# A graph layer's row picks by one-hot products: the one-hots as the moving side, the node table as the stationary one

## The chip, the cores and the metric

The kernel runs on one core of a Trainium2 chip. The metric is the device time of one execution in microseconds; three runs of the kernel before took 2540.1, 2541.27 and 2552.49 us, median 2541.27 us. The profile is of one more execution. Its columns name the engines: PE is TensorE's matmul, PEld TensorE's weight load, DVE VectorE, ACT ScalarE, POOL GpSimd, SP SyncE (which here only issues DMAs). A small q behind an engine's name is its queue of instructions, where waits and DMA issues stand.

## The reference

One message-passing layer on a graph with 6250 nodes and 206250 edges, 64 channels in 4 heads of 16, with a residual and a normalisation. The edges come sorted by destination.

```python
def reference(x, src, dst, edge_attr_64, Wq, bq, Wk, bk, We, be, Wv, bv):
    Qh = (x @ Wq.T + bq).reshape(n, H, D)
    Kh = (x @ Wk.T + bk).reshape(n, H, D)
    Vh = (x @ Wv.T + bv).reshape(n, H, D)
    Ee = (edge_attr_64 @ We.T + be).reshape(-1, H, D)
    score = (Kh[src] * Qh[dst] * (1.0 / np.sqrt(D)) * Ee).sum(-1)
    score = jnp.exp(jnp.clip(score, -5.0, 5.0))
    msg = Vh[src] * score[..., None]
    wV = jax.ops.segment_sum(msg, dst, num_segments=n).reshape(n, H * D)
    return _layernorm(x + wV, axis=-1)
```

## The kernel before

**Tiling.** An edge tile is 128 edges, one to a partition; 8 tiles are a group, 2 groups (16 tiles) a step. There are 105 steps: 97 of two groups and 8 of one group at the end. A step needs, for each edge, the key and value of its source node (128 numbers), the query of its destination node (64 numbers) and its edge term.

**Set-up.** Keys, values and queries of all nodes are computed once. Keys and values go to a table in DRAM (`kv_tab`), the queries, each split into three bf16 parts whose sum is the float32 value, to another (`q3_tab`). The node features themselves stay in SBUF as `parts`, also in three bf16 parts (call them high, middle and low), as 50 blocks of 128 nodes.

**Keys and values of an edge** come in two ways. Most tiles are gathered: GpSimd issues an indirect DMA per tile that fetches 128 rows of `kv_tab` (`gather_kv`, L443), four steps ahead of use into a ring of five steps' buffers. `gather` (L573) releases a step's gathers in six portions: a small copy of the source indices (`due_i`, L584 on VectorE or L586 on ScalarE) stands at a chosen place in that engine's order, and the gathers wait for it. Two tiles of each step, and three of every fifth (`THIRD`), 213 in all, are *picked* instead: their node features are taken out of `parts` by matmuls with one-hots, and then multiplied with the key and value weights. Picking a tile two steps ahead takes, in the names of the code:

- `sources` (L500, ScalarE): source index minus 50 times the column number, so that the number of the block appears in the column that belongs to the node's partition; `sources_turned` (L506, TensorE) transposes it into a PSUM bank, the tile `small`.
- `hots` (L516, VectorE): compares it with 25 block numbers at a time and writes one-hots, 25 blocks x 128 edges, two instructions per tile.
- `picks` (L530, TensorE): for each of the 50 blocks, a weight load of the one-hot (128 x 128) and a matmul that moves the 192 columns of the block's three parts past it; the 50 add up in PSUM (`rows3`, in the bank `pick`).
- `picked` (L544, VectorE) adds the three parts and copies out; `picked_turned` (L551, TensorE; L554, ScalarE) transposes; `picked_kv` (L564 to L571) multiplies with the weights, adds the bias by a matmul, and ScalarE copies the result into the ring.

**Queries of an edge** are spread by one-hots as well. Since edges are sorted by destination, the destinations of a group lie in a window of 42 nodes; `fetch_queries` (L187) loads that window's rows (42 nodes x 3 parts = 126 rows), `spread` (L594, TensorE) repeats the group's row of destination keys over the partitions into PSUM by two matmuls of 512 columns, `onehot_rows` (L616) and `onehot_rows_rest` (L621) make one-hots of it on ScalarE, and `queries` (L639) multiplies. Destination one-hots of the other kind (`onehot_edges`, L629) serve to add up the messages.

**One step** then runs: products (L646, L647) of keys, queries and edge terms on VectorE; scores (L653, L655, L656); messages (L663); a split of the messages into three bf16 parts, ScalarE copying a part (L666, L676) and TensorE subtracting it (`minus`, L674), twice; in the next step sixteen matmuls add the messages up by destination (`sums`, L682), and VectorE adds the result into a ring of accumulators (L696). Edge terms are eight float32 matmuls per step (`edge_values`, L432) onto a bias that ScalarE writes (L608).

**What sets the order.** Nothing is moved by a scheduler: every engine works off its instructions in the order in which the body of the loop over steps (L759 to L825) calls the functions above, and waits by semaphores where a tile is not ready or not free. The picks' work of a step is strewn over that body, so that TensorE has something between the links of the chain products, scores, messages, subtractions. PSUM's eight banks are all given out: `small`, `pick`, two each for `pe`, `pq` and `pb` (the spread keys, or a place for picked rows). Buffers for one-hots of picks: five.

## Time and profile before

| | us |
|---|---|
| median of three runs | 2541.27 |
| the profiled execution | 2551.2 |
| its span, first to last instruction | 2549.4 |
| set-up, to the first products | 134.2 |
| 97 steps of two groups begin between | 134.2 and 2443.9 |

The page gives busy times of each engine over the span; "by line" groups give the summed busy time, the mean of one instruction in ns and, behind the second bar, the engine's idle time just ahead of the group's instructions with what ended it. "Issue" there means that nothing the profile shows ended it, "remote" that a semaphore did whose setter could not be told. Rows of the windows' view read: stretch in us, its length, then busy us and number of instructions of PE, PEld, DVE, ACT and POOL, the granted share of TensorE's clock, the mean busy share of the DMA engines, and GB/s. Rows of the timeline read: start and duration in us, engine, line, operation, what is written and read, shape, number of instructions merged, and the idle time before it. Rows of the waits' view read: total us, times, longest.

### The profile page before, as it was taken

The numbers are of one execution on the slowest core, as the hardware profiler recorded it, in microseconds if no ns is written. First come the engines' busy times: TensorE is split into PE (matmuls) and PEld (weight loads), VectorE is DVE, ScalarE is ACT, GpSimd is POOL, SyncE is SP. The second block draws the span as 40 slices with busy tenths as digits, with TensorE's granted clock in tenths as the row PEclk, the third lists the DMA queues.
The fourth block names the chain that finished last, engine by engine and source line by source line (L and its number), as shares of the span: only waits on it lengthen the run. The fifth ranks groups of instructions, "written<-read, shape, count | busy, mean of one in ns | idle before, by whom it ended". The sixth has DMA issues, their size and how long they took to land.

```text
span 2549.4 us, 42602 instructions
## 1 busy us (share of the span) xinstructions
PE 1964.5 (77%) x17255; PEld 1623.3 (64%) x17255; DVE 1632.6 (64%) x2106; ACT 1029.6 (40%) x1778; POOL 1321.2 (52%) x1411
## 2 busy tenths in 40 slices
PE   4577877778877888777788787778778777777874
PEld 4466766666666666666666666667666666666663
DVE  3466766667666566676666666766767566666764
ACT  1344443434434344344343443444434343343544
POOL 5345555555555555555555555555555555555542
PEclk9988888988989888888888898888888898889985
DMA  4412222222222222222222222222222222222221
GB/s 119 125 41 66 56 67 63 59 65 65 65 57 54 65 65 58 72 65 57 64 66 55 64 58 66 62 60 56 70 69 56 64 68 55 66 62 55 64 57 35
DMA packets 104940, 163.05 MB, mean 64 GB/s; under 512 B 67130, under 2 KB 67454, under 8 KB 104622
## 3 DMA queue, kind: packets, MB, share of 16 engines
q0 software_dynamic: 44768, 90.73, 13.6%
q1 hardware_dynamic: 59582, 68.51, 9.5%
q8 instruction: 137, 2.24, 0.4%
q10 hardware_dynamic: 384, 1.00, 0.2%
q14 instruction: 69, 0.57, 0.1%
HBM read 152.79 MB, written 7.33 MB: 63 GB/s over the span
## 4 chain that ended last, share of the span: by engine, by line
PE 50%; issue 19%; POOL 10%; another core or an unknown queue 6%; DVE 5%; ACT 5%; DMA 0%; POOLq 0%; DVEq 0%; ACTq 0%
PE pick L530 25%; POOL kv L443 10%; PE pe L432 6%; PE pq L674 4%; PE pb L530 3%; PE small L682 3%; PE pb L594 2%; PE pb L566 2%; PE pq L639 2%; ACT msg L676 2%; DVE prod L646 1%; DVE prod L647 1%; DVE small L653 1%; PE pb L551 1%
## 5 line engine op out<-in xcount | busy, mean ns | idle before, releaser
L443 POOL DMA_INDIRECT kv<-kv_tab,due_i x1340 | 1263.7, 943 | 1149.3 <-DVE due_i L584 423.4
L530 PEld LDWEIGHTS <-hot 128*128 128x128 bf16 x10650 | 1002.3, 107 | 504.4 <-issue 431.7
L530 PE MATMUL pick<-parts,hot 128*128 128x192 bf16 x9700 | 1035.8, 265 | 298.7 <-issue 205.9
L516 DVE TENSOR_TENSOR hot<-small,block 128x3200 bf16<-128x3200 bf16 x426 | 755.5, 1815 | 18.4 <-remote 6.3
L616 ACT ACTIVATE to<-pb,minus_row 126x1024 bf16<-126x1024 f32 x202 | 224.0, 1109 | 842.4 <-PE pb L594 412.9
L646 DVE TENSOR_TENSOR prod<-kv,pq 128x1024 f32<-128x1024 f32 (+2 forms) x105 | 123.7, 1178 | 421.5 <-issue 148.6
L676 ACT ACTIVATE msg<-pq 128x1024 bf16<-128x1024 f32 (+2 forms) x210 | 207.2, 987 | 167.6 <-PE pb L551 81.4
L432 PEld LDWEIGHTS pe<-we_sb,et 128*128 128x128 f32 x1612 | 210.6, 207 | 86.1 <-ACT pe L608 64.2
L432 PE MATMUL pe<-we_sb,et 128*128 128x128 f32 x1612 | 226.2, 295 | 44.0 <-ACT pe L608 33.1
L621 ACT ACTIVATE to<-to,one_p 126x1024 bf16<-126x1024 bf16 x202 | 230.2, 1139 | 0.1
L682 PE MATMUL small<-msg,of 128*128 128x192 bf16 x1612 | 178.0, 262 | 33.2 <-issue 31.9
L544 DVE TENSOR_REDUCE xp<-pick 128x128 f32<-128x384 f32 x97 | 53.7, 554 | 203.7 <-remote 174.4
L674 PE MATMUL pq<-msg,minus_b 128*128 128x512 bf16 x404 | 132.7, 407 | 57.3 <-ACT msg L676 49.4
L682 PEld LDWEIGHTS <-of 128*128 128x128 bf16 x1612 | 146.6, 104 | 47.4 <-issue 45.2
L653 DVE TENSOR_REDUCE small<-prod 128x64 f32<-128x1024 f32 (+2 forms) x105 | 123.9, 1180 | 76.5 <-remote 34.6
L594 PE MATMUL pb<-key_rows,ident_b 112*128 112x512 bf16 x403 | 138.2, 423 | 23.9 <-ACT to L616 12.4
L530 PE MATMUL pb<-parts,hot 128*128 128x192 bf16 x950 | 116.7, 287 | 31.3 <-issue 31.1
L647 DVE TENSOR_TENSOR prod<-prod,pe 128x1024 f32<-128x1024 f32 (+2 forms) x105 | 123.6, 1177 | 4.0
L663 DVE TENSOR_TENSOR pq<-kv,small 128x1024 f32<-128x1024 f32 (+2 forms) x105 | 123.5, 1176 | 0.2 <-ACT small L656 0.2
L629 DVE TENSOR_TENSOR of<-small,key 128x2048 bf16<-128x2048 bf16 (+2 forms) x105 | 123.1, 1172 | 0.3
L571 ACT ACTIVATE kv<-pb 128x256 f32<-128x256 f32 (+1 forms) x97 | 39.2, 404 | 172.6 <-PE pb L566 51.7
L666 ACT ACTIVATE msg<-pq 128x1024 bf16<-128x1024 f32 (+2 forms) x105 | 103.8, 988 | 1.4 <-DVE pq L663 1.4
(140 smaller groups left out, 1321.1 us busy)
## 6 DMA issues: line engine op xcount, KB each, us to landing
et<-in_eT SPq DMA_DIRECT2D x100, 512.0 KB
kv<-kv_tab,due_i POOLq DMA_INDIRECT x1340
qw<-q_tab SPq DMA_DIRECT2D x202, 15.8 KB
kv_tab<-kv_sb SPq DMA_DIRECT2D x5, 640.0 KB
q_tab<-q SPq DMA_DIRECT2D x5, 480.0 KB
acc<-in_x SPq DMA_DIRECT2D x48, 32.0 KB
out<-y SPq DMA_DIRECT2D x48, 32.0 KB
xT_sb<-in_xT ACTq DMA_DIRECT2D x3, 320.0 KB
```

The costliest lines, as they stand in the source:

```text
L432: nc.tensor.matmul(pe[:, 2 * u:2 * u + 2, :], et[:, u, :], we_sb, start=False, stop=u == n // 2 - 1, skip_group_check=True)
L443: nc.gpsimd.indirect_dma_start(out=kv_of(g)[:, j, :], out_offset=None, in_=kv_tab[:, :], in_offset=bass.IndirectOffsetOnAxis(ap=of[:, t:t ...
L516: nc.vector.tensor_tensor(HOT[s, i, h].rearrange("p b (a c) -> p b a c", c=2), pairs(from_b[i])[:, None].to_broadcast(shape), block2[:, bl ...
L530: nc.tensor.matmul(to, hot[:, k, :], parts[:, b], start=b == 0, stop=b == NB - 1)
L594: nc.tensor.matmul(pb[:, b:b + 4, :], ident_b[:NR2, g // 2:g // 2 + 1].to_broadcast([NR2, P]), key_rows[:, g % 2, b * P:(b + 4) * P], star ...
L616: nc.scalar.activation(TO[g][:, :n, :], pb[:3 * W, :n, :], AF.Square, bias=minus_row3[:3 * W])
L621: nc.scalar.activation(TO[g][:, :n, :], TO[g][:, :n, :], AF.Relu, bias=one_p[:3 * W], scale=-1.0)
L646: nc.vector.tensor_mul(prod[:, :n, :], kvs[s % KVB][:, :n, :C], PQ[s][:, :n, :])
L653: nc.vector.tensor_reduce(score, prod[:, :n, :].rearrange("p g (h d) -> p g h d", h=H), axis=AX.X, op=OP.add)
L674: nc.tensor.matmul(msg[:, lo:hi, :], minus_b, M3[s][:, lo:hi, i, :], start=False, stop=True, skip_group_check=True)
L676: nc.scalar.activation(M3[s][:, :n, i + 1, :], msg[:, :n, :], AF.Copy)
L682: nc.tensor.matmul(PA[s], OH[s][:, j, :], M3[s][:, j], start=j == 0, stop=j == n - 1)
```

## The change

Picks are made for four tiles at a time, a batch of two steps' tiles, and the operands of the matmul change places.

- For each of the 50 blocks the stationary side is now a 128-column slice of `parts`, and the moving side the one-hots of all four tiles, 512 columns. Two matmuls per block: one whose slice holds the high and middle parts (into the bank `hi_mid`), one whose slice begins at the low part (into `low`; the upper 64 rows of that result, the next block's high part, are not read). A 51st block of zeros pads the table.
- The result has channels on the partitions and edges along the columns, which is how the next product needs it. So the reduction over the parts (L544) and the transposes (L551) go; ScalarE copies both banks out every second step (`picked`), and `picked_kv` multiplies, tile by tile, by weights stacked twice (`w2`: high and middle are added by the product itself) and by weights with the bias as a 65th row (`wb`). These are float32 matmuls.
- `hots` now writes 5 blocks x 512 edges; ten instructions per batch, five per step. `picks` runs in five portions per step, ten matmuls each.
- Batches run 0 to 46 (steps 0 to 93), three steps ahead: 188 tiles are picked, always the last two of a step; every-fifth-step thirds are gone.
- `spread` goes: the rows of destination keys are written to a DRAM table once (`key_tab`), and `fetch_keys` on SyncE's queue loads each group's row, repeated over 126 partitions, into one of four SBUF buffers two steps ahead. `onehot_rows` reads that.
- The sixth portion of a step's gathers is released by VectorE in place of ScalarE, and later in the body. The bank pair `pb` is given to `room`, where the picked keys and values are made, and `low`.
- In the other branch, which this input does not take, a tile of zeros is smaller.

The diff, without the parts that only rename or only touch set-up of tiles:

```diff
-LAST = NS - 8 - 1
+AHEAD = 3
+BATCH = 4
+LAST = (NS - 8 - AHEAD) // 2
+CUTS = 5
+NC = NB // CUTS // 2
...
+    key_tab = dram.tile([NR2, 2 * G * P], BF16, name="key_tab")
...
+            nc.sync.dma_start(key_tab, key_rows.rearrange("p i e -> p (i e)"))
...
+            def sources(m):
+                if m < LAST:
+                    for i in range(BATCH):
+                        FAR[m, i] = work.tile([P, P], BF16, name="far", bufs=BATCH)
+                        nc.scalar.activation(FAR[m, i], row50, AF.Identity, scale=-1.0,
+                                             bias=src_f[:, 2 * m + i // 2, i % 2:i % 2 + 1])
...
+            def hots(s, c):
+                if picks_in(s):
+                    b0 = (s % 2 * NC + c) * CUTS
+                    HOT[s, c] = work.tile([P, CUTS, BATCH * P], BF16, name="hot", bufs=5)
+                    shape = [P, CUTS, BATCH * P // 2, 2]
                     nc.vector.tensor_tensor(
-                        HOT[s, i, h].rearrange("p b (a c) -> p b a c", c=2),
-                        pairs(from_b[i])[:, None].to_broadcast(shape),
-                        block2[:, blocks(h), None, :].to_broadcast(shape), op=OP.is_equal)
+                        HOT[s, c].rearrange("p b (a c) -> p b a c", c=2),
+                        pairs(from_b)[:, None].to_broadcast(shape),
+                        block2[:, b0:b0 + CUTS, None, :].to_broadcast(shape), op=OP.is_equal)
...
-                    for k in range(NB // 2):
-                        b = h * NB // 2 + k
-                        nc.tensor.matmul(to, hot[:, k, :], parts[:, b], start=b == 0,
-                                         stop=b == NB - 1)
+                    for k in range(CUTS):
+                        b = (s % 2 * NC + c) * CUTS + k
+                        for i, to in ((0, hi_mid), (2, low)):
+                            at = (3 * b + i) * C
+                            nc.tensor.matmul(to, parts_flat[:, at:at + 2 * C], hot[:, k, :],
+                                             start=b == 0, stop=b == NB - 1)
...
             def picked(s):
-                if picks_in(s):
-                    X[s] = work.tile([P, 3, C], F32, name="xp")
-                    nc.vector.tensor_reduce(X[s][:, 1:], rows3.rearrange("p k i c -> p k c i"),
-                                            axis=AX.X, op=OP.add)
+                if s % 2 and picks_in(s):
+                    nc.scalar.activation(x2, hi_mid, AF.Copy)
+                    nc.scalar.activation(x1[:C], low[:C], AF.Copy)
+
+            def picked_kv(s, i):
+                if s % 2 and picks_in(s):
+                    to = s - 1 + AHEAD + i
+                    n = tiles_in(to)
+                    for j in range(2):
+                        es = slice((2 * i + j) * P, (2 * i + j + 1) * P)
+                        nc.tensor.matmul(rooms[:, j], x2[:, es], w2, start=j == 0, stop=False,
                                          skip_group_check=True)
+                        nc.tensor.matmul(rooms[:, j], x1[:, es], wb, start=False, stop=j == 1,
+                                         skip_group_check=True)
+                    nc.scalar.activation(kvs[to % KVB][:, n - 2:n, :], rooms, AF.Copy)
...
-                    if part < 3:
+                    if part not in (3, 4):
                         nc.vector.tensor_copy(due_i[:, due], src_i[:, due])
...
-            def spread(g):
-                pb = psum.tile([P, G, P], F32, name="pb")
-                for b in range(0, tiles_of(g), 4):
-                    nc.tensor.matmul(pb[:, b:b + 4, :],
-                                     ident_b[:NR2, g // 2:g // 2 + 1].to_broadcast([NR2, P]),
-                                     key_rows[:, g % 2, b * P:(b + 4) * P], start=True, stop=True)
-                return pb
+            def fetch_keys(g):
+                n = tiles_of(g) * P
+                KB[g] = work.tile([3 * W, G * P], BF16, name="kb", bufs=4)
+                nc.sync.dma_start(KB[g][:, :n], key_tab[g // 2:g // 2 + 1, g % 2 * G * P:][:, :n]
+                                  .to_broadcast([3 * W, n]))
...
+            def onehot_rows(g):
                 n = tiles_of(g)
                 TO[g] = work.tile([3 * W, G, P], BF16, name="to", bufs=4)
-                nc.scalar.activation(TO[g][:, :n, :], pb[:3 * W, :n, :], AF.Square,
-                                     bias=minus_row3[:3 * W])
+                nc.scalar.activation(TO[g][:, :n, :],
+                                     KB.pop(g)[:, :n * P].rearrange("p (j e) -> p j e", j=n),
+                                     AF.Square, bias=minus_row3[:3 * W])
```

and the body of the loop, with the calls in their new order (unchanged calls that stand between are left in):

```diff
                 if s + 2 < NS:
                     for g in groups_of(s + 2):
                         fetch_queries(g)
+                        fetch_keys(g)
                 if s:
                     sums(s - 1)
-                sources_turned(s, 1)
-                sources_turned(s + 1, 0)
-                sources_turned(s, 2)
+                picked(s - 1)
                 prod = products(s)
                 gather(s + KVB - 1, 0)
-                picked(s - 1)
-                picked_third(s - 1)
                 if more:
-                    onehot_rows(nexts[0], spread(nexts[0]))
-                picks(s, 0, 0)
+                    onehot_rows(nexts[0])
+                picks(s, 0)
                 score = scores(s, prod)
...
-                hots(s, 1, 0)
-                picks(s, 0, 1)
-                picked_turned(s - 1)
+                hots(s, 2)
+                picks(s, 1)
+                picked_kv(s - 1, 0)
                 minus(s, msg, 1)
                 gather(s + KVB - 1, 4)
...
-                hots(s, 1, 1)
-                picks(s, 1, 0)
-                picked_kv(s - 1)
-                gather(s + KVB - 1, 5)
-                sources(s + 1, 1)
-                sources(s + 2, 0)
-                sources(s + 1, 2)
+                hots(s, 3)
+                picks(s, 2)
+                if s % 2 == 0:
+                    sources((s + 2) // 2)
+                picked_kv(s - 1, 1)
+                hots(s, 4)
                 if more:
                     onehot_edges(s + 1)
                     queries(s + 1)
-                picks(s, 1, 1)
-                for h in range(2):
-                    hots(s, 2, h)
-                for h in range(2):
-                    picks(s, 2, h)
-                hots(s + 1, 0, 0)
-                hots(s + 1, 0, 1)
+                if s % 2:
+                    sources_turned((s + 1) // 2)
+                picks(s, 3)
+                hots(s + 1, 0)
+                gather(s + KVB - 1, 5)
+                picks(s, 4)
+                hots(s + 1, 1)
```

More of the change, by code (lines that the diff above doesn't have):

```diff
@@ L459, in tile_gnn @@
                 tc.tile_pool(name="psum", bufs=1, space=bass.MemoryType.PSUM) as psum:
-            TO, OH, PE, PQ, M3, PA = ({} for _ in range(6))
+            TO, OH, PE, PQ, M3, PA, KB = ({} for _ in range(7))
             small = fixed.tile([P, 4 * P], F32, name="small")
-            col, *from_b = (small[:, i * C:(i + 1) * C].bitcast(BF16) for i in range(4))
+            from_b = small[:, :4 * C].bitcast(BF16)
             score_all = small[:, 4 * C:4 * C + 2 * G * H]
             pa = small[:, 5 * C:8 * C].rearrange("p (i c) -> p i c", i=3)
+            room = fixed.tile([P, 4 * P], F32, name="room")
@@ L482, in tile_gnn @@
-            pick = fixed.tile([P, 4 * P], F32, name="pick")
-            rows3 = pick[:, :6 * C].rearrange("p (k i c) -> p k i c", k=2, i=3)
+                nc.vector.tensor_copy(src_f[:, :, i],
+                                      src_i[:, t0 + i:t0 + i + 2 * G * (2 * LAST - 1) + 1:2 * G])
+            hi_mid = fixed.tile([P, 4 * P], F32, name="pick")
+            low = fixed.tile([P, 4 * P], F32, name="low")
+            x2 = accp.tile([P, 4 * P], F32, name="x2")
+            x1 = accp.tile([C + 1, 4 * P], F32, name="x1")
@@ L504, in sources_turned @@
-            def sources_turned(s, i):
-                if wanted(s, i):
-                    nc.tensor.transpose(from_b[i], FAR.pop((s, i)), ident_b)
-            def blocks(h):
-                return slice(h * NB // 2, (h + 1) * NB // 2)
-            def hots(s, i, h):
-                if wanted(s, i):
-                    HOT[s, i, h] = work.tile([P, NB // 2, P], BF16, name="hot", bufs=5)
-                    shape = [P, NB // 2, P // 2, 2]
-                    nc.vector.tensor_tensor(
-                        HOT[s, i, h].rearrange("p b (a c) -> p b a c", c=2),
-                        pairs(from_b[i])[:, None].to_broadcast(shape),
-                        block2[:, blocks(h), None, :].to_broadcast(shape), op=OP.is_equal)
@@ new lines, in sources_turned @@
+            def sources_turned(m):
+                if m < LAST:
+                    for i in range(BATCH):
+                        nc.tensor.transpose(from_b[:, i * P:(i + 1) * P], FAR.pop((m, i)), ident_b)
+            def hots(s, c):
[3 more added lines that the diff above has]
+                    shape = [P, CUTS, BATCH * P // 2, 2]
+                    nc.vector.tensor_tensor(
+                        HOT[s, c].rearrange("p b (a c) -> p b a c", c=2),
+                        pairs(from_b)[:, None].to_broadcast(shape),
+                        block2[:, b0:b0 + CUTS, None, :].to_broadcast(shape), op=OP.is_equal)
@@ L578, in gather @@
                 lo, hi = PARTS[part] * n // 16, PARTS[part + 1] * n // 16
-                todo = [t for t in range(t0 + lo, t0 + hi) if not is_picked(t // G, t % G)
-                       ]
+                todo = [t for t in range(t0 + lo, t0 + hi) if not is_picked(t // G, t % G)]
                 if todo:
                     due = slice(todo[0], todo[-1] + 1)
-                    if part < 3:
+                    if part not in (3, 4):
                         nc.vector.tensor_copy(due_i[:, due], src_i[:, due])
@@ L744, in tile_gnn @@
             closed, scaled, normed = 0, 0, 0
-            sources(0, 0)
-            sources_turned(0, 0)
+            for g in range(4):
+                fetch_keys(g)
+            sources(0)
+            sources_turned(0)
             keys(0)
             for k, g in enumerate(groups_of(0)):
-                onehot_rows(g, spread(g))
+                onehot_rows(g)
                 onehot_rows_rest(g)
@@ L753, in tile_gnn @@
             onehot_edges(0)
-            sources(0, 1)
-            sources(1, 0)
-            sources(0, 2)
-            for h in range(2):
-                hots(0, 0, h)
+            for c in range(2):
+                hots(0, c)
             for s in range(NS):
```

97 lines of the change are left out of this document (24 added, 73 removed).

## The prediction

> **What bounds the kernel now.** I read the page first: busy shares, then the chain that ended last.
>
> ```profile
> span 2549.4 us, 42602 instructions
> PE 1964.5 (77%) x17255; PEld 1623.3 (64%) x17255; DVE 1632.6 (64%) x2106; ACT 1029.6 (40%) x1778; POOL 1321.2 (52%) x1411
> PE 50%; issue 19%; POOL 10%; another core or an unknown queue 6%; DVE 5%; ACT 5%; DMA 0%; POOLq 0%; DVEq 0%; ACTq 0%
> ```
>
> TensorE leads, but a fifth of the chain is "issue": an engine that waits for nothing the profile shows. How long is a step? One line's own view, and the timeline at the 97th step:
>
> ```profile
> L646 DVE TENSOR_TENSOR prod<-kv,pq x105: 421/1221/1223, 134.2 to 2536.2; 128x1024 f32<-128x1024 f32 x97, 128x512 f32<-128x512 f32 x7, 128x256 f32<-128x256 f32 x1
> 2443.87 1.21 DVE L646 TENSOR_TENSOR prod<-kv,pq 128x1024 f32<-128x1024 f32 x1
> ```
>
> 96 steps in 2443.9 - 134.2 = 2309.7 us: 24.06 us each, with 134 us ahead and 105.5 us of tail. Now the busy times by window; the counts behind the first two columns are TensorE's matmuls and weight loads:
>
> ```profile
> 134.20:2443.90 2309.70, 1835.74 (x16540) 1520.76 (x16540) 1525.75 (x1816) 947.22 (x1578) 1227.06 (x1302) 0.88 0.23 62
> 1226.60:1234.60 8.00, 6.94 (x49) 5.72 (x49) 5.35 (x10) 5.10 (x6) 3.53 (x4) 0.81 0.11 33
> 1230.20:1238.20 8.00, 7.07 (x68) 5.88 (x66) 7.76 (x11) 6.26 (x9) 5.67 (x6) 1.00 0.37 107
> 1238.20:1240.90 2.70, 0.82 (x7) 0.31 (x5) 2.66 (x2) 0.00 (x0) 0.94 (x1) 1.00 0.19 49
> 1251.90:1259.90 8.00, 7.27 (x59) 6.72 (x60) 2.57 (x7) 2.03 (x3) 0.63 (x1) 0.68 0.00 1
> 1258.60:1266.60 8.00, 7.93 (x78) 6.74 (x76) 7.76 (x11) 6.59 (x9) 5.65 (x6) 1.00 0.16 43
> 1266.60:1269.00 2.40, 0.79 (x6) 0.28 (x4) 2.40 (x2) 0.00 (x0) 0.94 (x1) 1.00 0.21 55
> ```
>
> 8 us with 134 instructions end in 2.7 us with 12; 8 us with 154 end in 2.4 us with 10; stretches with 98 and 119 run on. Over the loop TensorE takes 33080 / 2309.7 = 14.3 instructions per us, 345 a step. My reading: it can be fed some 14 to 15 per us for long, and what a burst takes above that it pays back in a pause. The pause spreads:
>
> ```profile
> 1219.06 2.23 PE L530 MATMUL pick<-parts,hot 128*128 128x192 bf16 x25
> 1221.13 1.48 PE L682 MATMUL small<-msg,of 128*128 128x192 bf16 x16
> 1226.12 0.56 DVE L544 TENSOR_REDUCE xp<-pick 128x128 f32<-128x384 f32 x1 [3.81 <-remote]
> 1226.73 3.65 PE L530 MATMUL pick<-parts,hot 128*128 128x192 bf16 x25 [2.95 <-issue]
> ```
>
> Picks recorded as done at 1221.3 are told to VectorE at 1226.1 only. Its reduction (L544) starts then, the next picks wait for it, and run at half rate: 3.65 us in place of 2.23, since the granted clock has fallen. The mean clock of 0.88 is a consequence, as is much of what the other engines' rows call "remote": they wait for TensorE's word, not for its work. So a step of 24.06 us is three things on TensorE: its streams of columns, the pauses, and the half clock after them; VectorE (15.9 us busy a step) and GpSimd follow.
>
> **The change, part by part** (per step unless said). Costs by group:
>
> ```profile
> L530 PEld LDWEIGHTS <-hot 128*128 128x128 bf16 x10650 | 1002.3, 107 | 504.4 <-issue 431.7 <-DVE prod L646 0.6
> L530 PE MATMUL pick<-parts,hot 128*128 128x192 bf16 x9700 | 1035.8, 265 | 298.7 <-issue 205.9 <-DVE xp L544 87.6 <-DVE prod L647 2.3
> L516 DVE TENSOR_TENSOR hot<-small,block 128x3200 bf16<-128x3200 bf16 x426 | 755.5, 1815 | 18.4 <-remote 6.3 <-issue 5.2 <-PE pick L530 3.3
> L629 DVE TENSOR_TENSOR of<-small,key 128x2048 bf16<-128x2048 bf16 x97 | 117.9, 1215 | 0.3
> L544 DVE TENSOR_REDUCE xp<-pick 128x128 f32<-128x384 f32 x97 | 53.7, 554 | 203.7 <-remote 174.4 <-PE pb L594 24.1 <-PE pick L530 3.6
> L594 PE MATMUL pb<-key_rows,ident_b 112*128 112x512 bf16 x403 | 138.2, 423 | 23.9 <-ACT to L616 12.4 <-issue 11.3
> L674 PE MATMUL pq<-msg,minus_b 128*128 128x512 bf16 x402 | 131.9, 408 | 54.6 <-ACT msg L676 48.9 <-issue 5.2 <-ACT msg L666 0.6
> L432 PEld LDWEIGHTS pe<-we_sb,et 128*128 128x128 f32 x1612 | 210.6, 207 | 86.1 <-ACT pe L608 64.2 <-issue 17.7 <-ACT to L621 0.3
> L443 POOL DMA_INDIRECT kv<-kv_tab,due_i x1340 | 1263.7, 943 | 1149.3 <-DVE due_i L584 423.4 <-issue 332.2 <-ACT due_i L586 326.3
> 1213.13 0.59 PE L674 MATMUL pq<-msg,minus_b 128*128 128x512 bf16 x2
> 1218.06 0.70 PE L566 MATMUL pb<-wkv,xe 128*128 128x256 f32 x2
> 1218.60 0.63 PE L639 MATMUL pq<-qw,to 126*128 126x64 bf16 x16
> 1222.62 0.94 POOL L443 DMA_INDIRECT kv<-kv_tab,due_i  x1 [0.30 <-issue]
> 1231.81 2.05 PE L432 MATMUL pe<-we_sb,et 128*128 128x128 f32 x16 [0.93 <-ACT pe L608]
> ```
>
> *Instructions of TensorE.* 10650 picks were 97 x 110; 47 batches x 100 are now 50 a step (94 steps). In load-and-multiply pairs: out go 110 picks, 4 spreads, 2 transposes of sources and some 5 of the transpose and key/value work; in come 50, 2, and 8 (four fp32 matmuls, two records each, as L432's 16 for eight show). 345 - 242 + 120 = 223. At 14.3 per us that is 15.6 us: no longer the bound. How fast is the feed without bursts? The trace bounds it only by this mean, which has the pauses in it, and from below by the 119 / 8 = 14.9 of the stretch that ran on. At 12 per us the 223 would still take 18.6, less than the sum below, so the choice within these bounds moves little. A batch's picks, two instructions per 0.22 us, come at 9 per us; bursts are left in sums, queries and edges, 32 instructions each.
>
> *Columns of TensorE.* From 25 and 16 matmuls of 192 columns: (2.23 - 1.48) / 9 = 0.083 us each, so 0.222 for 512 columns; two in 0.59, less one of 0.41, say 0.18. I take 0.222, the longer run. Picks: 50 x 0.222 = 11.1 (9.0 at 0.18) against 110 x 0.083 = 9.1: **dearer by 2.0**. The four spreads go (0.9). Key/value: four fp32 matmuls at 2.05 / 8 = 0.26 make 1.0, about what the bias matmul, L566's pair and the transposes took. Sum: picks 11.1, sums 16 x 0.083 = 1.3, queries 0.6, edges 2.05, minus 1.0, key/value 1.0, transposes 0.1 = 17.2 at full clock; the same for before, 16.1.
>
> The Trainium skill ("TensorE: Matmul & The Clock Gate", Back-to-back issue gap) gives about 216 ns for an isolated 512-column matmul but 131 ns sustained; at 131 the picks would be 6.6. No row here shows under 180, so the trace speaks for its first figure.
>
> The second matmul of each block computes 64 rows that nobody reads (the next block's first part), which is why 4/3 of the columns are paid for; the wider moving side saves weight loads that ran beside the multiplies anyway.
>
> *VectorE.* A one-hot of 2560 elements, between 2048 (1.215) and 3200 (1.815): 1.48; five make 7.4. Out: (755.5 + 53.7) / 97 = 8.3. One copy of indices comes over from ScalarE (0.2). Busy 1525.75 / 96 = 15.9 becomes 15.2. L544 no longer stands between picks and picks. What is late next on this engine is the chain products, scores, ScalarE's exponential, message: in order as before, and scores still wait for the sums, which share a bank with them. The four transposes of a batch's sources stand on TensorE behind the queries and wait for VectorE's fifth one-hot of the odd step; VectorE has then only the edges' one-hots (1.2 us) left before it needs their result, which the transposes, 0.3 us, meet. I take 0, from 0 to that 1.2 every second step.
>
> *GpSimd.* A gather takes 0.94 + 0.30 = 1.25 us. 188 tiles are picked in place of 213, so 14 gathers a step: **17.5 us** (17.3 before, hidden in 24). This becomes the tightest floor. The sixth release of indices moves from ScalarE behind VectorE's one-hots of the next step; behind it stands one more one-hot, and the copy waits for nothing, so its price is the 0.2 above.
>
> *ScalarE and the queues:*
>
> ```profile
> L676 ACT ACTIVATE msg<-pq 128x512 bf16<-128x512 f32 x14 | 8.4, 597 | 12.6 <-PE pq L674 12.6
> L571 ACT ACTIVATE kv<-pb 128x256 f32<-128x256 f32 x78 | 29.9, 383 | 144.1 <-PE pb L566 51.7 <-PE pq L639 42.1 <-PE pick L530 19.1
> L616 ACT ACTIVATE to<-pb,minus_row 126x1024 bf16<-126x1024 f32 x201 | 223.3, 1111 | 840.0 <-PE pb L594 410.6 <-remote 372.2 <-PE pick L530 41.9
> L621 ACT ACTIVATE to<-to,one_p 126x1024 bf16<-126x1024 bf16 x201 | 229.5, 1142 | 0.1
> 1219.12 1.08 SPq L187 DMA_DIRECT2D qw<-q_tab  x2
> DVE prod L646 <- DMA kv<-kv_tab,due_i: 39.7, 12, 6.4
> ```
>
> Every second step two evacuations of 512 columns, 2 x 0.6, of which the reading of hi_mid must be over before the next batch's first pick. Behind them on ScalarE stand the one-hots of the next step. On TensorE the sums (1.3 us) cover them; without that cover they cost 0.6 a step; I take 0.2. The four source rows of a batch now come in one step in place of two in each; ScalarE stays near 947.22 / 96 = 9.9, idle more than half the time, and that hides them. The squares read SBUF and wait for TensorE no more (L616's 410.6): 1.14 for 1.11. The keys' DMAs: two more issues on SyncE, some 1.1 us, two steps ahead, into buffers that ScalarE emptied a step before; behind them stands only the next step's loading. 252 packets of 2 KB, 516 KB a step, are as much again as the edges' loads, on a mean DMA share of 0.23. I take nothing, since waits for a gather's landing come to 39.7 us in the whole run (last row); the upper end is in rival 3. Start: a table written and read back before the first one-hots, +3 us (0 to 10), and three gathers more in a queue that has slack there.
>
> **Sum.** TensorE 17.2. Waits for others that stay: (64.2 + 48.9) / 97 = 1.2; the evacuation 0.2; pauses left over from short bursts (sums and queries together still come at over 14 per us), taken as a tenth of (431.7 + 205.9) / 97 = 6.6, i.e. 0.6. Bounds of the three: 0 to 2.5 for the waits (L544's 87.6 of picks' idle goes, but a like wait could come), 0 to 0.6, and 0 to 6.6; I stay near the low ends, since the counts above leave the bursts short and scattered. **19.2 us a step**, above GpSimd's 17.5. Between the marks of step 0 and step 96 are 94 steps with picks and two without (13 us each, an estimate: eight gathers at 1.25 and the chain of products and messages). In the tail step 96 picks no more, 2.5 us less. Span: 137 + 94 x 19.2 + 26 + 103 = 2071; in general 266 + 94 T. The profiled run is 2551.2, 2 above its span and 10 above the median of 2541.27, so the forecast is **2075**, about 18% off.
>
> **Rivals.**
> 1. *Pauses are not tied to the number of instructions.* For it: the profile names no releaser, and a load of edges or a run of gathers often lies near. Then pauses and cold clock stay and the columns cost: (17.2 - 16.1) / 0.88 = 1.25 more a step, 25.3: 266 + 94 x 25.3 = **2645, slower**. It decides if pauses come in 8-us stretches with fewer than 120 instructions. Against it: the windows above. A rule on its side: the Trainium skill ("Runtime: NRT & Kernel Launch", Instruction fetch mechanics) holds that fetching is hidden by an issue floor of some 20 cycles, so that the count would not matter. Chance 0.09.
> 2. *GpSimd's floor.* The pauses vanish with their waits, T = 17.5 to 18.2: **1911 to 1977**. For it: TensorE's 17.2 lies just below. Against it: gathers are released piecemeal by copies on VectorE and ScalarE (423.4 + 326.3 us of idle). Chance 0.15.
> 3. *Half the pauses stay,* or the keys' DMAs bring a like loss: +3 us, T = 20.3 to 23.3, middle **2315**. Chance 0.19.
> 4. *Nothing comes of it:* a new wait eats the gain, within 0.5% of 2541. Chance 0.03.
>
> **How the numbers follow.** Forecast (T 18.2 to 20.3, 1977 to 2174): 0.54. The range takes in the upper 0.7 of rival 2 (T from 17.7) and the lower 0.8 of rival 3 (T to 22.7): 1930 to 2400, which holds 0.54 + 0.11 + 0.15 = 0.8. Measurements of this kernel tell about 0.5% from no change. Faster: 0.54 + 0.15 + 0.19 = 0.88; same 0.03; slower 0.09.
>
> **What would show it.** Right: L530's idle by "issue" under 100 us; granted clock above 0.95; some 223 TensorE instructions a step; picks 0.22 apart; GpSimd above 60% busy. Wrong: pauses of 0.7 us and more inside the picks' runs; picks cold at 0.43; one-hots waiting for the keys' DMA; key/value products waiting for late gathers.

## The result, and the profile after

The kernel after took 2463.76 us (median of four, 2458.75 to 2469.47) against 2546.88 us before (four, 2540.1 to 2554.36): ratio 0.967, 95% interval 0.963 to 0.972. Faster, as foreseen, but by 3.3% where 18% was foreseen, and above the range. In three later sets of runs, one on another chip and two on a chip that gave the long times in other sets, the kernel before took about 1790 us; the kernel after, run in one of them, took 1988 us, a ratio of 1.112 (1.107 to 1.116): there the change is a loss. One execution of the kernel before in the last of these sets took 2368.39 us, at a granted clock of 0.66 where its other executions have 0.97; it is left out of that set's ratios.

First the page of the kernel after, from the set of the 0.967:

```profile
span 2457.0 us, 30837 instructions
PE 1852.5 (75%) x11184; PEld 1101.6 (45%) x11184; DVE 1504.8 (61%) x2122; ACT 1034.2 (42%) x1627; POOL 1345.5 (55%) x1436
issue 24%; PE 20%; POOL 16%; ACT 15%; another core or an unknown queue 12%; DVE 10%; DMA 2%; DVEq 0%; POOLq 0%; SPq 0%; ACTq 0%
L518 PE MATMUL pick<-hot,parts 128*128 128x512 bf16 x2350 | 937.8, 399 | 3.8 <-issue 3.8
L506 DVE TENSOR_TENSOR hot<-small,block 128x2560 bf16<-128x2560 bf16 x470 | 679.4, 1481 | 337.6 <-PE small L498 250.1
L518 PEld LDWEIGHTS <-parts 128*128 128x128 bf16 x4700 | 473.0, 102 | 581.7 <-issue 120.7
```

TensorE's pauses inside the picks are nearly gone: 3.8 us of idle by issue on the multiplies and 120.7 on the loads, where L530 had 205.9 and 431.7. Yet the chain has more issue than before, and no engine is busy for more than 75%. The windows' row of the 96 steps between the first and the 97th product:

```profile
147.22:2359.41 2212.19, 1730.15 (x10614) 1004.82 (x10613) 1403.25 (x1843) 951.80 (x1435) 1248.19 (x1323) 0.93 0.32 88
```

A step takes 2212.19 / 96 = 23.04 us, for 24.06 before. TensorE is busy for 18.02 of it (19.12 before) and idle for 5.02 (4.94 before). So only the busy part shrank, with the granted clock up from 0.88 to 0.93; the pauses' time came back as waits. Which ones, the waits' view says; five of its rows (total us, times, longest):

```profile
DVE hot L506 <- PE small L498: 250.1, 34, 9.0
ACT x L524 <- PE pick L518: 238.7, 35, 8.3
ACT msg L639 <- remote: 235.9, 57, 6.3
PE pq L637 <- ACT msg L639: 137.8, 44, 4.2
PE pe L431 <- ACT pe L571: 118.6, 45, 10.1
```

Three of the five are ScalarE or VectorE waiting for TensorE. (Of these, the second is no sign of trouble: in run c_after, told below, it is 268.3, while the first is 107.9 there.) The third close up, in the timeline (rows of TensorE, ScalarE and GpSimd):

```profile
1205.85 0.59 PE L637 MATMUL pq<-msg,minus_b 128*128 128x512 bf16 x2
1208.23 0.38 PE L518 MATMUL low<-hot,parts 128*128 128x512 bf16 x1
1209.23 1.02 ACT L639 ACTIVATE msg<-pq 128x1024 bf16<-128x1024 f32 x1 [3.61 <-remote]
1205.92 0.95 POOL L442 DMA_INDIRECT kv<-kv_tab,due_i  x1 [0.30 <-ACT to L584]
1207.17 0.94 POOL L442 DMA_INDIRECT kv<-kv_tab,due_i  x1 [0.30 <-issue]
1210.62 0.94 POOL L442 DMA_INDIRECT kv<-kv_tab,due_i  x1 [2.50 <-ACT due_i L551]
```

The second subtraction ends at 1206.44, and TensorE goes on: the pick at 1208.23 is the tenth that it starts behind it. ScalarE, idle since 1205.6, begins the copy at 1209.23, 2.8 us later. TensorE's word (the update of its semaphore, by which the others learn that a result is there) came late: the trace has the update itself at 1209.21, 1.1 us after the end (1208.11) of a run of gathers that stood back to back. The same place in the same kernel, in a set in which the kernel before took 1790 us (run c_after, below):

```profile
1211.32 0.59 PE L637 MATMUL pq<-msg,minus_b 128*128 128x512 bf16 x2
1211.76 0.38 PE L518 MATMUL pick<-hot,parts 128*128 128x512 bf16 x1
1211.97 0.38 PE L518 MATMUL low<-hot,parts 128*128 128x512 bf16 x1
1211.95 1.02 ACT L639 ACTIVATE msg<-pq 128x1024 bf16<-128x1024 f32 x1 [0.19 <-PE pq L637]
1210.41 0.94 POOL L442 DMA_INDIRECT kv<-kv_tab,due_i  x1 [0.30 <-issue]
1211.65 0.94 POOL L442 DMA_INDIRECT kv<-kv_tab,due_i  x1 [0.30 <-issue]
```

The gathers are as dense, and the word takes 0.04 us. I call the first *late* sets and the second *prompt* ones. The next table takes the subtractions at whose modelled end ScalarE was free: mean time from that end to the copy's start, us (number), by how many gathers GpSimd began in the 6 us before that end.

```
gathers begun in 6 us       0-1         2          3          4          5
before                   0.04 (8)   0.04 (9)   0.04 (6)   1.46 (20)  0.92 (15)
after                    0.04 (8)   0.04 (4)   0.04 (4)   0.09 (11)  1.00 (42)
after, half the gathers  0.04 (35)  0.04 (105) 0.04 (1)   0.04 (1)       -
after, prompt set        0.04 (8)   0.04 (3)       -      0.04 (23)  0.04 (109)
VectorE to ScalarE, after 0.10 (4)  0.09 (8)   0.09 (32)  0.09 (41)  0.09 (17)
```

The last row is VectorE's clip (L618) to ScalarE's exponential (L619): that word is never late. Only TensorE's is, and never below four gathers in 6 us. The traces also hold the times of the semaphores' updates themselves, and they say the same. The next table counts, of each engine's updates on record in the 96 steps, those that stand over 0.5 us behind the end of the last of its instructions that makes one (in brackets the longest, us).

```
                    TensorE           VectorE       ScalarE
before          730 of 1809 (8.5)    0 of 1172     0 of 1139
after           423 of 1338 (6.8)    0 of 990      0 of 840
a_half_rows     423 of 1331 (6.2)    0 of 927      0 of 851
a_half_gathers    7 of 1431 (5.5)    0 of 1482     0 of 1295
a_no_gather       6 of 1537 (4.8)    0 of 1482     0 of 1278
a_pool_busy       2 of 1539 (5.0)    0 of 1607     0 of 1315
c_after           0 of 1513 (0.02)   0 of 1619     0 of 1316
```

(The runs named with a_ and c_ follow in the next section. In the three that leave gathers out, the longest, 4.8 to 5.5 us, stand at the loop's first run of 14 gathers, which they keep.)

### The profile page after: what moved, and what is told of

Read it like the earlier page. It is cut to its first block, busy times and chain, and to the rows that moved or that the text cites. A ratio compares the mean times of both kernels' runs of the same rounds, so it can differ in the third digit from the quotient of the medians.

```text
span 2457.0 us, 30837 instructions
## 1 busy us (share of the span) xinstructions
PE 1852.5 (75%) x11184; PEld 1101.6 (45%) x11184; DVE 1504.8 (61%) x2122; ACT 1034.2 (42%) x1627; POOL 1345.5 (55%) x1436
## 4 chain that ended last, share of the span: by engine, by line
issue 24%; PE 20%; POOL 16%; ACT 15%; another core or an unknown queue 12%; DVE 10%; DMA 2%; DVEq 0%; POOLq 0%; SPq 0%; ACTq 0%
POOL kv L442 16%; PE pick L518 4%; PE low L518 4%; ACT msg L639 4%; PE pe L431 4%; ACT to L584 3%; ACT to L578 2%; PE pq L637 2%; DVE small L616 2%; DVE hot L506 2%; ACT pe L571 2%; DVE prod L610 2%; DVE prod L609 2%; ACT msg L629 1%
## 5 line engine op out<-in xcount | busy, mean ns | idle before, releaser
L518 PE MATMUL pick<-hot,parts 128*128 128x512 bf16 x2350 | 937.8, 399 | 3.8 <-issue 3.8
L518 PE MATMUL low<-hot,parts 128*128 128x512 bf16 x2350 | 933.3, 397 | 1.9 <-issue 1.6
L506 DVE TENSOR_TENSOR hot<-small,block 128x2560 bf16<-128x2560 bf16 x470 | 679.4, 1481 | 337.6 <-PE small L498 250.1
L518 PEld LDWEIGHTS <-parts 128*128 128x128 bf16 x4700 | 473.0, 102 | 581.7 <-issue 120.7
L431 PE MATMUL pe<-we_sb,et 128*128 128x128 f32 x1612 | 255.6, 323 | 251.5 <-ACT pe L571 118.6
L592 DVE TENSOR_TENSOR of<-room,key 128x2048 bf16<-128x2048 bf16 (+2 forms) x105 | 123.4, 1175 | 361.4 <-ACT far L492 180.5
L639 ACT ACTIVATE msg<-pq 128x1024 bf16<-128x1024 f32 (+2 forms) x210 | 207.4, 988 | 307.5 <-remote 235.9
L619 ACT ACTIVATE small<-small 128x64 f32<-128x64 f32 (+2 forms) x105 | 21.6, 206 | 511.9 <-DVE due_i L549 291.8
L578 ACT ACTIVATE to<-kb,minus_row 126x1024 bf16<-126x1024 bf16 x202 | 229.8, 1138 | 7.7 <-DMA kb<-key_tab 4.6
L637 PEld LDWEIGHTS <-minus_b 128*128 128x128 bf16 x404 | 43.3, 107 | 166.3 <-issue 155.0
L533 PE MATMUL room<-w,x 128*128 128x128 f32 x376 | 76.0, 284 | 51.3 <-ACT kv L537 51.3
```

Of the source, the lines that this page charges most:

```text
L431: nc.tensor.matmul(pe[:, 2 * u:2 * u + 2, :], et[:, u, :], we_sb, start=False, stop=u == n // 2 - 1, skip_group_check=True)
L506: nc.vector.tensor_tensor(HOT[s, c].rearrange("p b (a c) -> p b a c", c=2), pairs(from_b)[:, None].to_broadcast(shape), block2[:, b0:b0 + ...
L518: nc.tensor.matmul(to, parts_flat[:, at:at + 2 * C], hot[:, k, :], start=b == 0, stop=b == NB - 1)
L578: nc.scalar.activation(TO[g][:, :n, :], KB.pop(g)[:, :n * P].rearrange("p (j e) -> p j e", j=n), AF.Square, bias=minus_row3[:3 * W])
L637: nc.tensor.matmul(msg[:, lo:hi, :], minus_b, M3[s][:, lo:hi, i, :], start=False, stop=True, skip_group_check=True)
L639: nc.scalar.activation(M3[s][:, :n, i + 1, :], msg[:, :n, :], AF.Copy)
```

## The experiments

Theory A: dense gathers of GpSimd hold back TensorE's word to the other engines (and, it may be where its queue fills, TensorE itself). Theory B: the bursts of the hardware queue do, the keys' rows above all. Theory C, the prediction's: the number of TensorE's instructions alone brings the pauses.

**First set (late; before 2576.8 us, median of seven).** Gathers left out after the fifth step's, in both kernels; every second left out; the keys' rows loaded once:

```diff
                 for t in todo:
-                    gather_kv(t // G, t % G, due_i)
+                    if s < KVB:                 # a_no_gather, b_no_gather
+                        gather_kv(t // G, t % G, due_i)
...
+                    if s < KVB or t % 2:        # a_half_gathers
...
+                if g >= 4:                      # a_no_keydma, in fetch_keys
+                    KB[g] = KB0[g % 4]
+                    return
```

> The kernel after, but from the sixth step on no row is gathered in the loop (the copies that release them stay); keys and values are then those of earlier steps. Theory A (runs of gathers on GpSimd hold back TensorE's word to the other engines): with no gathers the word comes at once, gaps of TensorE that end in a wait fall from 5.9 us a step to about 1.5, T falls from 22.9 to 17.5 to 19 us, time 1910 to 2060 us. Theory B (the bursts of the hardware queue, the keys' rows above all, hold it back): waits stay, T 22 or more, time above 2350. A third possibility, that landing gathers are what the engines wait for, gives the same fall in time as A, but the delays of the word would then be short in the kernel after already, which its trace speaks against.

> The kernel before with the same omission. Theory A: TensorE's pauses inside the picks' runs go with the gathers (3.5 us a step now), the picks' idle by issue falls from 432 us to under 60, although TensorE still has 345 instructions a step; T 17 to 19.5 us in place of 24.06, time 1870 to 2110. Theory C (the prediction's: the number of TensorE's instructions alone brings the pauses, 14 to 15 per us for long): pauses and T stay, idle by issue above 350 us, time above 2450.

> The kernel after with every second gather of the loop left out (7 a step in place of 14). Theory A: runs of gathers are half as long (mean 3 to 4 in place of 5 to 6), few words of TensorE are over 1 us late, T 18.5 to 20.5 us, time 2000 to 2200. If only GpSimd's busy time as such counted (a floor of 17.5 us a step), the time would fall as far as with none left. Theory B: no fall, above 2350.

> The kernel after, but the keys' rows are loaded for the first four groups alone and used for all later groups, so that 516 KB a step less go over the hardware queue; the one-hots of rows are then those of other edges. Theory B: the word comes in time, T 18 to 20, time 1960 to 2150. Theory A: time within 2 per cent of 2464, 2415 to 2500, with TensorE's waits as they were.

Measured: 2019.57, 1812.85, 2053.22 and 2485.43 us (the last with a ratio to before of 0.965, 0.960 to 0.970, as the kernel after has it). B falls. So does C, and thoroughly. The kernel before without gathers, windows of its 96 steps:

```profile
145.94:1719.76 1573.82, 1532.64 (x16540) 1357.29 (x16539) 1505.84 (x1815) 942.99 (x1576) 13.24 (x14) 0.99 0.14 37
```

and its picks on the page:

```profile
L530 PEld LDWEIGHTS <-hot 128*128 128x128 bf16 x10650 | 887.2, 98 | 105.4 <-issue 40.3
L530 PE MATMUL pick<-parts,hot 128*128 128x192 bf16 x9700 | 867.8, 246 | 28.2 <-DVE xp L544 24.5
```

33079 instructions in 1573.82 us are 21 per us, against the 14 to 15 that I had taken for the most TensorE can be fed; idle by issue is 40.3 where it was 431.7, and the clock is 0.99. The pauses of the kernel before came with the gathers. In the kernel after, half the gathers cost hardly more time than none (2053 against 2020): at two or three in 6 us no word is late, which speaks for their density. Nor were these executions prompt ones by chance. Their set-ups, which keep all their gathers, lasted 141.0 to 149.7 us, as in late sets (85 to 88 in prompt ones), and in a_no_gather's ScalarE waited up to 10.12 us for TensorE's first results:

```profile
34.30 0.38 ACT L330 ACTIVATE kv_sb<-ps 128x256 f32<-128x256 f32 x1 [10.12 <-remote]
```

The kernel after without gathers, and the one with keys loaded once:

```profile
140.99:1930.02 1789.03, 1601.06 (x10426) 974.75 (x10613) 1398.96 (x1843) 954.92 (x1435) 13.20 (x14) 0.97 0.20 60
```

```profile
147.71:2381.06 2233.35, 1724.97 (x10426) 1012.11 (x10613) 1403.92 (x1843) 952.60 (x1435) 1251.36 (x1323) 0.92 0.24 64
```

Without gathers a step is 18.64 us in the kernel after, 16.39 in the kernel before: the change itself costs 2.25.

**Second set (late; on a second chip; before 2549.89, ten).** What of a gather does it, and can the runs be broken up?

```diff
+                        nc.gpsimd.indirect_dma_start(    # a_half_rows: 256 bytes a row
+                            out=kv_of(g)[:, t % G, :C], out_offset=None,
+                            in_=kv_tab.rearrange("n (i c) -> (n i) c", i=2),
...
+                        nc.gpsimd.tensor_copy(key_rows[:, 0, :512],    # a_pool_busy
+                            due_i[:NR2, t:t + 1].to_broadcast([NR2, 512]))
...
-                    gather_kv(t // G, t % G, due_i)      # a_no_release: no copies to due_i
+                    gather_kv(t // G, t % G)
...
-PARTS = 0, 2, 4, 7, 9, 11, 16
+PARTS = tuple(range(17))                                 # a_single: 16 places of release
```

> The kernel after, but the loop's gathers fetch rows of 256 bytes in place of 512 (the keys' half alone, from wrong rows; the messages use old values): as many gathers and rows, half the bytes. If the bytes that land hold TensorE's word back (theory A1): delays as with half the gathers, time 2030 to 2150. If the number of rows or of gathers does (A2: their descriptors, or GpSimd's back-to-back issue): word as late as in the kernel after, time 2400 to 2500.

> The kernel after with each gather of the loop replaced by a GpSimd copy of 512 numbers that waits for the same release, so GpSimd is as busy in runs, but moves nothing by DMA. If a busy GpSimd as such holds the word back: time 2300 or more. If it is the gathers' DMA work (A): time as without gathers, 2000 to 2080, unless a copy takes far over 1 us, when GpSimd itself would set the pace.

> The kernel after with the gathers of a step released at once, when their buffer is free, without the copies of indices: one run of 14 gathers (17.5 us) a step in place of some three runs. Theory A: TensorE's word is late for most of the step; time 2500 to 2750, slower than after. A rival by which GpSimd's waiting for its releases is what costs (750 us of its idle time): T near GpSimd's 17.5 to 19, time 1930 to 2050.

> The kernel after with every gather released by a copy of its own, spread over the step (14 releases in place of 6), so that runs become shorter; all work is done. Theory A: mean length of a run under 4, fewer words over 1 us late, time 2250 to 2420 (copies cost VectorE and ScalarE some 0.8 us each a step). If the density of gathers counts and not the runs: no gain, 2450 to 2520.

Measured: 2464.43, 2034.74, 2826.16 us and, for a_single, 2519.3 (ratio 0.989, 0.986 to 0.992). Half the bytes change nothing. GpSimd working without DMA does not hold the word back, though its copies took less than a gather's 944 ns, from the group's row:

```profile
L556 POOL CAST key_rows<-due_i 112x512 bf16<-112x512 int32 x1348 | 831.1, 617 | 994.3 <-DVE due_i L549 645.4 <-ACT due_i L551 300.8
```

One run of 14 gathers a step is worse by 360 us than six releases, more than A foresaw. a_single is a **miss**: runs did get shorter (83 of the loop's 357 were single gathers, in the kernel after 20 of 313), but with GpSimd needed for 17.5 us of every step the density stayed, words came 2 us late and more in runs of three too, and by its ratio it lost some 55 us against after, of which its added copies may be a part. Breaking up runs is no cure; what fits all runs is density, not the length of a run.

**Third set (prompt; a third chip; before 1793.74, thirteen) and fourth (prompt; the first set's chip; before 1790.16, thirteen).**

```diff
+                            out=kv_of(g)[:P // 2, t % G, :], out_offset=None,   # a_half_count, d_half_count
+                            in_offset=bass.IndirectOffsetOnAxis(ap=due_i[:P // 2, t:t + 1], axis=0))
...
-PARTS = 0, 2, 4, 7, 9, 11, 16
+PARTS = 0, 0, 0, 0, 0, 16, 16                    # a_late, d_late
...
             def spread(g):                       # b_keys, d_keys, e_keys: the kernel before
+                return KB.pop(g)[:, :tiles_of(g) * P].rearrange("p (j e) -> p j e", j=tiles_of(g))
...
+                        fetch_keys(g)
```

(The keys' rows take three buffers there, for want of room.)

> The kernel after, but each gather of the loop fetches 64 rows (half the partitions) in place of 128; as many gathers, half the rows; the other half keeps old values. If the number of rows in flight holds TensorE's word back (B1): time as with half the gathers, 2030 to 2150. If it is the number of gather instructions in a row (B2): 2400 to 2500. A gather that takes less time on GpSimd with fewer rows would leave gaps between gathers and speak for neither by itself.

> The kernel after with all 14 gathers of a step released by one copy on ScalarE, behind the second subtraction, so that the one run of 17.5 us covers the end of the step and the start of the next and leaves the chain of score, message and subtractions free. If only TensorE's words of that chain cost time: 2250 to 2400. If the words at the step's end (queries to products, transposes to one-hots, sums to scores) cost as much: 2450 to 2700.

> The kernel before with one part of the change alone: the keys' rows spread by DMA from DRAM, the picks as before. Its four matmuls of 512 columns (0.9 us) and eight instructions a step go from TensorE, and ScalarE's squares wait for TensorE no more. Theory A: a small part of the gain, 0 to 1.5 us a step, ratio to before 0.95 to 1.0. If the whole gain of the change were this part: ratio 0.96 to 0.97.

> The kernel after itself, unchanged, once more beside the kernel before. The last set (a_half_count, a_late, b_keys) ran on another chip, on which the kernel before took 1794 us and TensorE's word was never late. If the chip is again of that sort: after 1980 to 2060, ratio 1.10 to 1.15, since there the change's own cost is left (2020 against 1813 without gathers). If it is of the first sort: ratio 0.96 to 0.975 as at first.

> Gathers of 64 rows in place of 128, as in a_half_count. On a chip of the first sort (before near 2550): 2030 to 2150 if the number of rows in flight holds TensorE's word back, 2400 to 2500 if the number of gather instructions does. On one of the second sort: about 1990 and no news.

> One release of all 14 gathers behind the second subtraction, as in a_late. On a chip of the first sort: 2250 to 2400 if the words of the chain score, message, subtractions are those that cost, 2450 to 2700 if those at the step's end cost as much. On one of the second sort: 1975 to 1990 as measured, and against after it tells whether fewer releases gain anything there.

> The kernel before with the keys' rows spread by DMA alone, as in b_keys. On a chip of the first sort: ratio to before 0.95 to 1.0 (0.96 to 0.97 if the whole gain of the change is this part). On one of the second sort: 0.996 to 1.0 as measured.

Measured in the third set: 1988.23, 1982.1 (ratio 1.105, 1.102 to 1.108) and 1790.59 (0.998, 0.996 to 1.000); in the fourth c_after 1987.6 (1.112, 1.107 to 1.116), 1985.42, 1983.23 (1.109, 1.105 to 1.113) and 1789.59 (1.000, 0.998 to 1.001). No word was late in any of them, although all gathers were made and stood back to back. Windows of c_after's steps, and of its page the span and the edges' matmuls:

```profile
85.27:1897.65 1812.38, 1626.27 (x10614) 984.97 (x10613) 1403.68 (x1843) 955.25 (x1435) 1247.71 (x1323) 0.96 0.38 107
```

```profile
span 1987.5 us, 30837 instructions
L431 PE MATMUL pe<-we_sb,et 128*128 128x128 f32 x1612 | 259.0, 326 | 204.3 <-ACT pe L571 204.3
```

18.88 us a step, what a_no_gather has in a late set (18.64). So the gathers cost next to nothing of themselves; what they cost in late sets is the word. The questions these runs were meant for (rows or instructions, which words matter, the keys' share of the gain) can be asked only where words are late, so these runs are **inconclusive** on them. What they show is that keys by DMA alone neither gain nor lose where words are prompt, and that the picks of the kernel before then run without the pauses, all gathers made: idle by issue is 95.9 us in b_keys, where the kernel before had 431.7 in a late set.

```profile
L532 PEld LDWEIGHTS <-hot 128*128 128x128 bf16 x10650 | 890.3, 98 | 143.9 <-issue 95.9
L649 DVE TENSOR_TENSOR prod<-kv,pq x105: 422/1220/1222, 86.0 to 1775.1; 128x1024 f32<-128x1024 f32 x97, 128x512 f32<-128x512 f32 x7, 128x256 f32<-128x256 f32 x1
1697.32 1.22 DVE L649 TENSOR_TENSOR prod<-kv,pq 128x1024 f32<-128x1024 f32 x1 [1.40 <-PE pick L532]
```

The last two rows are its first and its 97th product: (1697.32 - 86.0) / 96 = 16.78 us a step.

The late word is at work from the start of the kernel: the set-up issues 32 gathers in a row while ScalarE copies TensorE's first results. In the late set:

```profile
14.72 1.23 PE L328 MATMUL ps<-w_sb,xT_sb 65*128 65x128 f32 x4 [0.47 <-issue]
22.71 0.39 ACT L330 ACTIVATE kv_sb<-ps 128x256 f32<-128x256 f32 x1 [8.04 <-remote]
```

and in c_after:

```profile
7.76 0.38 ACT L330 ACTIVATE kv_sb<-ps 128x256 f32<-128x256 f32 x1 [0.47 <-PE ps L328]
```

ScalarE's idle time before such a copy is 8.04 us in the one and 0.47 in the other. The set-up lasts 147.2 us in the one, 85.3 in the other: in a trace of these kernels the first 30 us tell the sort of set.

**Fifth set (late; same chip; before 2573.12, seven) and sixth (prompt; same chip; before 1793.61, twelve).** Is the change's own 2.25 us the wait ahead of the edges' matmuls, 204.3 us in c_after and 14.6 in b_no_gather?

```diff
                 picks(s, 0)
+                picks(s, 1)
                 score = scores(s, prod)
...
                 hots(s, 2)
-                picks(s, 1)
+                picks(s, 2)
```

(and picks 3 and 4 one place up as well)

> The kernel after with the second share of a step's picks moved ahead of the edges' matmuls (and each later share one place up): its one-hots are ready from the step before, and TensorE now stands about 2 us a step at the edges' matmuls, waiting for ScalarE's biases (204 us of the run in c_after). If this wait is what makes after's step 2 us longer than before's where no word is late: T 16.7 to 17.6 there (GpSimd's 14 gathers set 17.5), time 1830 to 1930, ratio to before 1.02 to 1.08 in place of 1.11. If the columns of the picks are all of it: no change, ratio 1.10 to 1.12. Where words are late (before near 2550): 2330 to 2470, ratio 0.91 to 0.97.

> The kernel before with the keys' rows spread by DMA alone, a third time. Where the kernel before takes near 2550 (late words): ratio 0.95 to 1.0 if the keys are a part of the change's gain, 0.96 to 0.97 if they are all of it, over 1.0 if the gain is that of the turned picks alone. Where it takes near 1790: 0.996 to 1.002 as twice measured.

> The kernel after with the second share of picks ahead of the edges' matmuls, once more. Where the kernel before takes near 1790: 1830 to 1930, ratio 1.02 to 1.08, if the wait for the biases is what makes the step 2 us longer, 1.10 to 1.12 if not. Where it takes near 2550: ratio 0.96 to 0.965 as in f_shift.

Measured: f_shift 2478.36 (ratio 0.963, 0.960 to 0.965; not to be told from after's 0.967), e_keys 1793.27 (1.000, 0.999 to 1.002), e_shift 1959.67 (1.094, 1.091 to 1.096): 28 us less than c_after and far from the 60 to 160 expected. The waits of e_shift say why:

```profile
PE small L645 <- DVE hot L506: 131.4, 92, 2.0
PE pe L431 <- ACT pe L571: 68.4, 49, 6.5
```

TensorE's wait for biases fell by 136 us (204.3 to 68.4), and the sums, now reached earlier, wait 131 us for VectorE's one-hots, a row that c_after doesn't have: the sums' bank, `small`, holds the sources that the one-hots read. The edit moved the wait by a few places. Where words are prompt, no complete version here beats the kernel before; where they are late, none beats the kernel after.

## Why the prediction was wrong, point by point

- **The step that failed: "it can be fed some 14 to 15 per us for long, and what a burst takes above that it pays back in a pause".** b_no_gather was fed 21 per us for 1574 us nearly without pauses. My windows compared counts of instructions and never asked what GpSimd did in them. Their own rows held the answer: the stretches that ended in a pause had 6 gathers' worth of GpSimd's time (5.67 and 5.65 us of 8), those that ran on 3.53 and 0.63. What brings the pauses is the gathers' density where words are late: without gathers idle by issue was 40.3 us, with them and prompt words 95.9, in place of 431.7.
- **Its consequence.** From it followed that fewer instructions would free the step of 24.06 us. By windows, in us a step: before 24.06 (busy 19.12, idle 4.94), without gathers 16.39 (15.96 and 0.43), so gathers cost 7.7 there. After 23.04 (18.02 and 5.02), without gathers 18.64 (16.68 and 1.96), so they cost 4.4. Nearly all of it is late words: with prompt words and all gathers the steps take 16.78 (b_keys, as fast as the kernel before in its set) and 18.88 (c_after), only 0.4 and 0.2 more than without gathers. The net gain of 1.0 is 3.3 that the gathers cost less, and 2.25 of the change's own cost. The pauses did go, as foretold; the word stayed late, and "waits for others that stay", taken as 1.2, became an idle time of 5. Why the kernel after suffers less, fewer instructions to fill TensorE's queue or fewer words to wait for, no run separates. That it came out faster at all is luck of the set: where words are prompt it is 11% slower.
- **Rival 1** had the premise right (pauses not tied to the count, runs of gathers near) and the price wrong, since it let the pauses stay. Its test, pauses in stretches with under 120 instructions, would not have found them in the windows shown. A queue that fills while the word is held would make count and pause go together; that is argued, not shown.
- **Rival 3** has the measured step in its band (23.04 of 20.3 to 23.3), but by another road: not half the pauses stayed, the waits for late words took their place.
- **The terms of the sum** were near. TensorE's instructions: (10614 + 10613) / 96 = 221 a step, foreseen 223. Picks start 0.21 to 0.22 us apart (1211.76 and 1211.97), as taken; the 131 ns that the Trainium skill ("TensorE: Matmul & The Clock Gate", Back-to-back issue gap) states for sustained ones doesn't show in the prompt set either. One-hots 1481 ns for 1.48. The busy difference of the two kernels without gathers is 0.72, columns foretold 1.1. Where words are prompt the step is 18.88 for 19.2. What was mis-sized there too is the wait on ScalarE's biases, 204.3 / 96 = 2.1 us (a_no_gather 191.5 / 96 = 2.0; b_no_gather 0.15).
- **The keys' DMAs cost nothing:** right; a_no_keydma gains nothing by dropping 516 KB a step.
- **Set-up +3:** it was +13 (147.2 for 134.2), but that says little: late runs with the set-up of the kernel after took 138.6 to 152.3. With prompt words the set-ups with a key table took 85.3 to 87.8, whichever kernel they stood in; that the +13 is late words as well is argued, not shown.
- **Of the signs to look for,** 221 instructions and 0.22 us came, the picks' idle by issue nearly (3.8 and 120.7 for under 100); the clock (0.93 for over 0.95) and GpSimd's share (55% for over 60%) didn't. In c_after both did (0.96; 68%): the forecast described the kernel after in a prompt set, and took its gain from a kernel before in a late one.

## What to carry to other kernels

Where an engine waits for "remote" or "issue" after another has ended its work, list what every other engine and queue was doing at that moment before a cause is given to a count that merely goes along; leaving out the suspect is the quick test (b_no_gather moved 30% of the time). And before a change is believed, measure both kernels more than once, at other times: here the verdict turned from 3% faster to 11% slower with a condition that neither kernel sets.

## What the runs showed of the hardware

- In some sets of runs TensorE's completion signals reach the other engines late (in the steps of the kernel after 225 of 1338 by over 2 us, the longest 6.8), while GpSimd issues gathers at four or more in 6 us. VectorE's signals in the same trace take 0.1 us. The Trainium skill ("SBUF — State Buffer", Who interferes with whom) says "PE and ACT never wait on anyone"; that speaks of ports, but what TensorE has done became known late here, and in the kernel before TensorE itself paused.
- The bytes of a row don't matter (2464.43 us with 256 bytes in the second set, 2463.76 with 512 in the very first), nor does GpSimd's being busy with copies (2034.74); the gathers' density does.
- Whether the word is late changes between sets on one chip (before 2577 and 2573 us, 1790 and 1794 us). What brings it about, and whether rows or gather instructions count, stays open.
- Records go missing along with it: in the steps of the kernel after 990 of VectorE's 1621 updates are on record in the late trace, 1619 in c_after. Every execution timed here was recorded while it ran. Whether the recording has a part in the late word, or only loses records by the same cause, no run here shows.
